# A two-layer graph network: GpSimd clears 256 columns behind every gather, VectorE and ScalarE fetch some chunks by columns, and eleven row buffers are used

## The chip, the cores and the metric

The kernel runs on one core of a Trainium2 chip. The metric is the time of one execution on the device in microseconds (us); lower is better. A core has five engines that run side by side, each with its own instructions in program order, and they wait for one another by semaphores: TensorE (PE: matrix products and transposes into PSUM), VectorE (DVE) and ScalarE (ACT) for work element by element, GpSimd (POOL), and SyncE (SP), which issues DMAs. Here GpSimd issues the indirect DMAs, which fetch rows of a table in device memory by a list of indices.

## The reference

12,500 nodes with 128 features each and 200,000 edges sorted by destination. Layer 1 takes a maximum over the edges of a node, layer 2 a sum.

```python
h = jnp.maximum(_layernorm(x, axis=-1), 0.0)
wsum = segment_sum(edge_weight, dst)
w = edge_weight / jnp.maximum(wsum, EPS)[dst]
feat = relu(h @ W_pool + b_pool)
neigh = segment_max(feat[src] * w[:, None], dst)
neigh = where(deg[:, None] > 0, neigh, 0.0)
rst = h @ W1_self + neigh @ W1_neigh + b1
h1 = relu(rst / jnp.maximum(norm(rst), EPS))
neigh2 = segment_sum(h1[src] * w[:, None], dst) / jnp.maximum(deg, 1.0)[:, None]
out = x + relu(h1 @ W2_self + neigh2 @ W2_neigh + b2)
```

## The kernel before

The edges go in 391 groups of 512 (`G`), each of four chunks of 128 (`Q`). Three stages follow one another.

**Preparation.** The normalised features h are built by columns (feature on the partition, node along the row) in the wide tile `one_way`, which stays on the chip; feat goes to device memory as the table `feat_d`. The first 17 groups (`FIRST`) gather rows of x and finish them themselves, so that layer 1 starts before the table is whole. A generator, `source_steps`, builds the index lists `srcT`.

**Layer 1.** One turn of the loop for each group. `gather` (L513) has GpSimd issue four indirect DMAs, one for a chunk, from `feat_d` into a row buffer `gt` of 128 x 4 x 128. TensorE transposes the chunks into PSUM (`pm`, L964); VectorE multiplies by the edge weights (L1006), runs a scan that takes the maximum along each node's edges (L979), makes a selection (`sel`, L990) and compacts (L999, L1002); TensorE turns the compacted columns (`two_pr`, L1019), ScalarE copies them (`rows`, L974), TensorE multiplies by `sel` (L1028) and ScalarE copies the result to the group's place in a wide tile, at an address that it loaded into a register (L914; registers at L735). VectorE works on several groups' steps in one turn: the program is written as a pipeline, with `due(k)` naming the group k turns back. Work of four nodes' tiles at a time (L796 to L824) turns the result into h1, stored as table `h_d` and kept by columns in `other_way`.

**Layer 2.** GpSimd gathers four chunks of `h_d`; TensorE multiplies each by a small matrix `s` (L1075) that VectorE made from the places and weights (L1063, L1068); VectorE adds the product `pa` to the running sums at a register address (L1080).

What sets the order around the change: each engine's instructions stand in program order; GpSimd's are nearly all gathers. A gather waits until its row buffer is free, that is, until TensorE has read the group that lay there before. `buffer` names the row buffer: layer 1 has a ring of 18 buffers in borrowed space (`ring`), later 14 (`mid`), and from about group 113 the tiles of `full`; layer 2 has `full` alone. `full` holds 11 tiles (`RING` + `MORE`), of which `buffer` uses four (`DEEP`).

Of the kernel before, what the change touches and what calls it, by code (L numbers as in the profile page):

```python
# [7 lines left out]
F32 = mybir.dt.float32  # L8
# [10 lines left out]
P = 128  # L19
# [19 lines left out]
LEAST = LESS + 4 * MID  # L39
KEPT = 4  # L40
# [6 lines left out]
DEEP = 4  # L47
# [3 lines left out]
def gnn_kernel(ctx, tc, x, src, dst, ew, w_pool, b_pool, w1s, w1n, b1, w2s, w2n, b2, out):  # L51
# [31 lines left out]
    s_d = dram.tile([2, NP], F32, name="s_d")  # L83

# [13 lines left out]
    bp_all, b1_all, b2_all = (const.tile([P, D], F32, name=f"b_{i}") for i in range(3))  # L98
    ident = const.tile([P, P], F32)
# [106 lines left out]
    ones_w = rp.tile([P, P], F32)  # L206
    nc.vector.memset(ones_w, 1.0)
# [20 lines left out]
    diff = wk.tile([P, P], F32, bufs=1)  # L228
    nc.gpsimd.iota(diff, pattern=[[1, P]], base=0, channel_multiplier=-1,
# [9 lines left out]
    nc.vector.tensor_scalar(ident, diff, 0.0, None, op0=OP.is_equal)  # L239
    shift = {}  # L240
    for name, at in (("up", 1), ("up_wrap", 1 - P), ("down", -1), ("down_wrap", P - 1)):
        shift[name] = rp.tile([P, P], F32, name=f"shift_{name}")
        nc.vector.tensor_scalar(shift[name], diff, float(at), None, op0=OP.is_equal)
# [264 lines left out]
    def gather(gt, table_d, g, only=None, last=None):  # L508

        t, r, ne, chunks = edges_of(g)  # L510
        limit = {} if last is None else dict(bounds_check=last, oob_is_err=False)
        for j, k in chunks if only is None else chunks[only:only + 1]:
            nc.gpsimd.indirect_dma_start(  # L513
                out=gt[:k, j, :], out_offset=None, in_=table_d[:, :],
                in_offset=bass.IndirectOffsetOnAxis(ap=srcT[:k, t, j, r:r + 1], axis=0), **limit)
        return gt
# [94 lines left out]
    for i in range(len(groups) + 3):  # L611
# [46 lines left out]
        if i < 2 or 9 <= i < 21:  # L658
            next(source_steps, None)
# [31 lines left out]
    def background():  # L691

        for t in range(1, NT):
            yield P * t - 2 * KEPT, edges1, t
        for t in range(NT):
            yield NG, edges2, t
        for t in reversed(range(NT)):
            yield NG, edges3, t
        for t in range(NT):
            yield NG, fitness, t  # L700
        yield NG, lambda get, t: verdict(get), 0

# [168 lines left out]
    with tc.manual_schedule(), tc.tile_pool(name="ew", bufs=3) as wk, \  # L871
# [12 lines left out]
        pms, scs, sels, prs, rws, pas = ({} for _ in range(6))  # L884
        two_pr = ps.tile([P, 2, Q // 2, D], F32, bufs=1)
# [47 lines left out]
        for i in range(max(turn) + 6):  # L933
            if i == NG - 8:
# [9 lines left out]
            if FIRST <= i < NG:  # L944
                gts[i] = gather(buffer(i, True), feat_d, i)
# [5 lines left out]
            if i < FIRST:  # L951
                if i > 0:
                    nc.scalar.activation(pms[i], raws.pop(i).rearrange("p q n -> p (q n)"), AF.Relu, bias=bp_col)
                if i + 1 < FIRST:
                    raw_columns(pn, i + 1)
                if i + 2 < FIRST:
                    raw_scale(i + 2)
                    raw_norm(i + 2)
                if i + 1 < FIRST:
                    raw_back(i + 1)  # L960
            elif i < NG:
                gt = gts.pop(i)
                for j, k in reversed(edges_of(i)[3]):
                    nc.tensor.transpose(pms[i][:, j * P:j * P + k], gt[:k, j, :], ident[:k, :k])  # L964
# [17 lines left out]
            if due(3) is not None:  # L982
                t, r, _, chunks = pairs_of(due(3))
                sel = sels[due(3)] = wk.tile([P, Q // 2, LW], F32, name="sel")
# [7 lines left out]

            pick()
# [47 lines left out]
            if i >= FIRST and i % 3:  # L1041
                side_step()
        assert not busy
# [6 lines left out]
    with tc.manual_schedule(), tc.tile_pool(name="ew2", bufs=3) as wk, \  # L1050
# [6 lines left out]

        nc.vector.memset(agg2, 0.0)
# [66 lines left out]
        for i in range(max(turn) + 2):  # L1125
            if EARLY <= i < NG:
                gts[i] = gather(buffer(i, False), h_d, i)
                places(i)
            if EARLY <= i < NG:
                weighted(i)  # L1130
# [9 lines left out]
            quad_stage(3)  # L1140
            if i in turn:
# [20 lines left out]
            if EARLY <= g < NG:  # L1162
                window_add(g, window_at(mybir.EngineType.DVE, g))
        assert late is None and not quads
# [121 lines left out]
```

## Time and profile before

| | us |
|---|---|
| median of 3 runs | 4587.56 |
| lowest, highest | 4581.83, 4592.94 |
| the profiled execution | 4582.98 |
| its span in the profile | 4581.2 |
| gathers of layer 2 | from about 2372 to 4568 |

The profile is of one execution. A group row of it reads: line, engine, operation, written tile <- read tiles, count | busy us, mean ns of one | idle time of the engine just before them, and what ended most of that. "issue" is waiting for which the profile shows no cause; "remote" is waiting that ended at a semaphore whose giver the profile can't name for that moment. A row of the timeline is: start, duration, engine, line, operation, tiles, and in brackets the idle time ahead of it and what ended it. PE is TensorE's products, PEld its weight loads, which overlap them. A small suffix q (ACTq, DVEq) marks an engine's sequencer, which handles registers and their loads.

### The profile page before, as it was taken

Reading aid. Unit: us, or ns where it says so; the run is one execution under the profiler, and the core shown is the slowest. Engines: PE = TensorE matmul, PEld = TensorE weight load, DVE = VectorE, ACT = ScalarE, POOL = GpSimd, SP = SyncE. Lnnn points to the kernel's source line nnn. Section 1 sums busy time; section 2 is a strip of 40 time slices with the busy share of each in tenths; the row PEclk is TensorE's granted clock in tenths of the full one; section 3 lists DMA queues with packets and bytes.
Section 4 is the critical chain, followed back from the end, with each engine's and each line's share of the span. In section 5 each row is a group of like instructions: output and inputs, shape, how many; then the busy total and the mean of one; then the engine's idle time right before and its main releaser. Section 6 shows DMA issues by size and latency. Waiting matters only on the chain.

```text
span 4581.2 us, 30093 instructions
## 1 busy us (share of the span) xinstructions
PE 1950.3 (43%) x8086; PEld 1623.2 (35%) x8086; DVE 1759.1 (38%) x4405; ACT 422.1 (9%) x1257; POOL 2963.4 (65%) x3143
## 2 busy tenths in 40 slices
PE   3554444444344444443444443333333333333333
PEld 2443334333333333332344433333333333333333
DVE  3676667666666666665561111111111111111111
ACT  3531111111111111111110000000000000000000
POOL 5366664666666666666666666666666666666665
PEclk7765555555555555555555555555555555555555
DMA  4344444444444444443431122211121112112111
GB/s 134 107 117 122 127 120 117 117 119 120 117 119 117 117 120 118 118 121 113 120 96 48 46 57 55 54 51 51 50 56 51 51 51 55 52 51 56 51 51 51
DMA packets 193262, 396.94 MB, mean 87 GB/s; under 512 B 60623, under 2 KB 63822, under 8 KB 193088
## 3 DMA queue, kind: packets, MB, share of 16 engines
q0 software_dynamic: 100032, 204.97, 17.3%
q1 hardware_dynamic: 92320, 189.06, 13.6%
q8 instruction: 69, 1.13, 0.1%
q10 hardware_dynamic: 736, 0.92, 0.1%
q14 instruction: 105, 0.86, 0.1%
HBM read 374.96 MB, written 19.77 MB: 86 GB/s over the span
## 4 chain that ended last, share of the span: by engine, by line
POOL 29%; issue 26%; another core or an unknown queue 19%; DVE 13%; PE 11%; ACT 2%; DMA 1%; POOLq 0%; ACTq 0%; DVEq 0%
POOL gt L513 28%; DVE pm L979 4%; PE pm L964 3%; PE pn L1028 2%; DVE pm L1006 2%; PE two_pr L1019 2%; DVE sc L999 1%; DVE sq L816 1%; DVE sc L1002 1%; DMA gt<-h_d,srcT 1%; PE pa L1075 1%; PE pf L649 1%; ACT rows L974 1%; DVE sel L990 0%
## 5 line engine op out<-in xcount | busy, mean ns | idle before, releaser
L513 POOL DMA_INDIRECT gt<-h_d,srcT x1551 | 1467.7, 946 | 728.9 <-issue 414.2
L513 POOL DMA_INDIRECT gt<-feat_d,srcT x1303 | 1234.9, 948 | 671.8 <-issue 360.7
L1075 PE MATMUL pa<-s,gt 128*128 128x24 f32 x3102 | 716.7, 383 | 1260.4 <-DMA gt<-h_d,srcT 803.5
L1075 PEld LDWEIGHTS pa<-s,gt 128*128 128x128 f32 x3102 | 687.4, 325 | 1328.0 <-issue 813.2
L1080 DVE TENSOR_TENSOR way<-pa,way 128x41 f32 x391 | 77.7, 199 | 1726.2 <-remote 1016.0
L1019 PE MATMUL two_pr<-ident,sc 128*128 128x128 f32 x782 | 243.9, 412 | 942.4 <-ACT rows L974 557.2
L1006 DVE TENSOR_TENSOR pm<-pm,gs 128x512 f32<-128x512 f32 x390 | 271.8, 697 | 680.7 <-remote 428.4
L979 DVE TENSOR_TENSOR_SCAN pm<-kt,pm 128x512 f32<-128x512 bf16 x389 | 499.0, 1283 | 7.1
L1019 PEld LDWEIGHTS two_pr<-ident,sc 128*128 128x128 f32 x782 | 124.9, 201 | 1055.3 <-ACT rows L974 596.0
L964 PE MATMUL pm<-ident,gt 128*128 128x128 f32 x1303 | 323.8, 397 | 99.5 <-issue 54.3
L1028 PEld LDWEIGHTS pn<-sel,rows 128*128 128x128 f32 x1564 | 350.2, 308 | 0.2
L1028 PE MATMUL pn<-sel,rows 128*128 128x48 f32 x1564 | 334.7, 359 | 0.0
L964 PEld LDWEIGHTS pm<-ident,gt 128*128 128x128 f32 x1303 | 243.0, 222 | 135.3 <-issue 87.8
L974 ACT ACTIVATE rows<-two_pr 128x256 f32<-128x256 f32 x392 | 150.4, 384 | 1515.1 <-remote 1046.2
L990 DVE TENSOR_SCALAR sel<-cols,lastT,invT 128x48 f32<-128x48 f32 x782 | 253.4, 324 | 0.0
L832 ACT ACTIVATE oT<-pn,b_col 128x512 f32<-128x512 f32 x24 | 16.5, 689 | 2181.5 <-PE pn L797 701.8
L999 DVE COPY sc<-pm 128x256 f32<-128x256 f32 x391 | 165.8, 424 | 78.8 <-remote 67.3
L1002 DVE COPY_PREDICATED sc<-kt,pm 128x256 f32<-128x256 int16 x389 | 169.3, 435 | 3.9 <-remote 3.9
L513 POOL DMA_INDIRECT w2T<-feat_d,srcT x100 | 94.7, 947 | 97.8 <-DVE raw_mv L527 50.8
L1068 DVE TENSOR_TENSOR s<-place,w2T 128x96 f32<-128x96 f32 x391 | 100.8, 258 | 74.9 <-remote 35.0
L1063 DVE TENSOR_TENSOR place<-place,locT 128x96 f32<-128x96 f32 x391 | 100.9, 258 | 0.3 <-DVE way L1080 0.3
L914 ACT ACTIVATE way<-pn 128x48 f32 x391 | 81.8, 209 | 120.8 <-issue 46.9
(288 smaller groups left out, 1622.8 us busy)
## 6 DMA issues: line engine op xcount, KB each, us to landing
gs<-in_edge_weight SPq DMA_DIRECT2D x389, 256.0 KB
kt<-keep_d SPq DMA_DIRECT2D x97, 512.0 KB
gt<-h_d,srcT POOLq DMA_INDIRECT x1551
gt<-feat_d,srcT POOLq DMA_INDIRECT x1303
feat_d<-fr SPq DMA_DIRECT2D x24, 256.0 KB
xr<-in_x SPq DMA_DIRECT2D x24, 256.0 KB
out<-o SPq DMA_DIRECT2D x24, 256.0 KB
h_d<-sq SPq DMA_DIRECT2D x23, 256.0 KB
```

The lines of the kernel that those rows point to most:

```text
L513: nc.gpsimd.indirect_dma_start(out=gt[:k, j, :], out_offset=None, in_=table_d[:, :], in_offset=bass.IndirectOffsetOnAxis(ap=srcT[:k, t, j, ...
L964: nc.tensor.transpose(pms[i][:, j * P:j * P + k], gt[:k, j, :], ident[:k, :k])
L974: nc.scalar.activation(rws[g][:k, j, :], pr[:k, j, :], AF.Copy)
L979: nc.vector.tensor_tensor_scan(pm[:, :ne], kt[:, :ne], pm[:, :ne], carry, op0=OP.add, op1=OP.max)
L990: nc.vector.tensor_scalar(part, cols[:k, 1, :], lastT[:k, t, j, r:r + 1], invT[:k, t, j, r:r + 1], op0=OP.is_equal, op1=OP.mult)
L999: nc.vector.tensor_copy(sc[:, :ne // 2], two[:, :, 1])
L1002: nc.vector.copy_predicated(sc[:, :ne // 2], new[:, :, 1], two[:, :, 0])
L1006: nc.vector.tensor_tensor(pms[i][:, :n], rows[:, :n], ws.pop(i)[:, :n], OP.mult)
L1019: nc.tensor.transpose(prs[g][:k, j, :], sc[:, j * P:j * P + k], ident)
L1028: nc.tensor.matmul(pas[g], rows[:k, j, :], sel[:k, j, :], start=j == 0, stop=j == len(chunks) - 1)
L1063: nc.vector.tensor_tensor(hit, iota, locT[:, t, :, r:r + 1].to_broadcast([P, Q, PART]), OP.is_equal)
L1075: nc.tensor.matmul(pas[g][:, PART_AT[j]:PART_AT[j] + PART], gt[:k, j, :], s[:k, j, :], start=j == len(chunks) - 1, stop=j == 0, skip_group ...
```

## The change

- Behind every gather, except those of the group 0, GpSimd writes zeros to a tile `spare` of 128 x 256; nothing reads them.
- `buffer` uses all 11 tiles of `full` in both layers.
- A class `Columns` fetches single chunks without GpSimd. The table by columns is on the chip anyway (`one_way` for layer 1, `other_way` for layer 2), and one edge is one column of it. For each chunk SyncE brings a list row with 128 byte addresses (from `at_d`, written in the preparation); the fetching engine loads 16 of them into registers at a time (L755) and copies column after column from the register addresses into the row buffer's slot. ScalarE copies one column with each instruction (128 a chunk, L793). VectorE writes two with each (64 a chunk, L805), the first of them negated.
- Layer 1: VectorE fetches chunk 1 of each 8th group from group 33 on, ScalarE chunk 3 of each 4th from group 29. The columns are of h, not of feat, so TensorE multiplies by `W_pool` instead of a transpose (L1006) and ScalarE adds the bias and cuts at zero (L1011).
- Layer 2: VectorE fetches chunk 1 of each 3rd group from 13 on, ScalarE chunk 2 of each 3.75th. TensorE turns the chunk (`flip`, L1206) and ScalarE copies it back, with the signs put right for VectorE's.
- The preparation computes the address lists (L510). The shift matrices become views of one wider tile, and a bias tile shares its space with `spare`.

In all 361 chunks are fetched by columns (170 by VectorE, 191 by ScalarE), and 2765 gathers are left of 3126.

```diff
+TABLES_AT = (8320, 58688)
+BURST = 16
-DEEP = 4
+REST = 256
...
         if not wide:
-            return full[g % DEEP]
+            return full[g % len(full)]
...
-        return mid[(h - LESS) % MID] if h < LEAST else full[(h - LEAST) % DEEP]
+        return mid[(h - LESS) % MID] if h < LEAST else full[(h - LEAST) % len(full)]
...
             nc.scalar.activation(srcT[:, t], pt, AF.Copy)
+            for layer in range(2):
+                row = (layer * NT + t) * P
+                place = wk.tile([P, G], I32, name="sa")
+                nc.vector.tensor_scalar(place, sr[:, t, :], 4.0, float(TABLES_AT[layer]), op0=OP.mult, op1=OP.add)
+                nc.sync.dma_start(at_d[row:row + P, :], place)
+                yield
...
-    def gather(gt, table_d, g, only=None, last=None):
+    def gather(gt, table_d, g, only=None, last=None, besides=()):
...
         for j, k in chunks if only is None else chunks[only:only + 1]:
+            if any(c.j == j and c.takes(g) for c in besides):
+                continue
             nc.gpsimd.indirect_dma_start(
...
+            if table_d is not x or g > 0:
+                nc.gpsimd.memset(spare, 0.0)
...
+        def load(self, g, _):
+            row = self.layer * NT * P + g
+            nc.sync.dma_start(self.lists[self.place[g]], at_d[row:row + 1, self.j * P:(self.j + 1) * P])
+            self.ready.add(g)
...
+    def one_by_one(slot, r, columns_read):
+        for e, column in enumerate(columns_read, r):
+            by_scalar(slot[:, e:e + 1], column)
...
+    def two_by_two(slot, r, columns_read):
+
+        for e in range(0, BURST, 2):
+            nc.vector.scalar_tensor_tensor(slot[:, r + e:r + e + 2], zero_high, columns_read[e],
+                                           columns_read[e + 1].to_broadcast([P, 2]),
+                                           op0=OP.subtract, op1=OP.min)
...
+        for k, engine, copy, j, every, first in ((0, mybir.EngineType.DVE, two_by_two, 1, 8, FIRST + 16), (1, mybir.EngineType.Activation, one_by_one, 3, 4, FIRST + 12),):
...
-                gts[i] = gather(buffer(i, True), feat_d, i)
+                gts[i] = gather(buffer(i, True), feat_d, i, besides=bycol)
...
+                for c in bycol:
+                    c.turn(i, c.multiplied, c.cut)
                 for j, k in reversed(edges_of(i)[3]):
+                    if any(c.j == j and c.takes(i) for c in bycol):
+                        continue
                     nc.tensor.transpose(pms[i][:, j * P:j * P + k], gt[:k, j, :], ident[:k, :k])
...
+            for c in bycol:
+                c.turn(i, c.load, c.fetch)
...
+        for k, engine, copy, j, every, first in ((0, mybir.EngineType.DVE, two_by_two, 1, 3, 13), (1, mybir.EngineType.Activation, one_by_one, 2, 3.75, 13),):
```

How this moves the instructions. GpSimd in the middle of layer 2, before (`gt_98` and so on are the row buffers; the brackets hold the semaphores that an instruction waits for):

```order
L513 DMA gt_98<-h_d,srcT 128x128 [waits DMASW4_49]
L513 DMA gt_98<-h_d,srcT 128x128 [waits DMASW5_49]
L513 DMA gt_98<-h_d,srcT 128x128 [waits DMASW6_49]
L513 DMA gt_99<-h_d,srcT 128x128 [waits DMASW7_49,PE_49]
L513 DMA gt_99<-h_d,srcT 128x128 [waits DMASW0_49]
L513 DMA gt_99<-h_d,srcT 128x128 [waits DMASW1_49]
```

and now:

```order
L527 DMA gt_106<-h_d,srcT 128x128 [waits DMASW5_49,PE_49]
L531 MEMSET spare 128x256 [waits Pool_49]
L527 DMA gt_106<-h_d,srcT 128x128 [waits DMASW6_49]
L531 MEMSET spare 128x256 [waits Pool_49]
L527 DMA gt_106<-h_d,srcT 128x128 [waits DMASW7_49]
L531 MEMSET spare 128x256 [waits Pool_49]
```

Between two gathers stands a memset, which waits for the memset before it; only a group's first gather waits for TensorE, as before.

VectorE in layer 1, before:

```order
L1006 TENSOR_TENSOR pm<-pm,gs 128x512
L979 SCALAR_TENSOR_TENSOR pm<-kt,pm 128x512
L990 TENSOR_SCALAR sel<-cols,lastT,invT 128x48
L999 COPY sc<-pm 128x256
L990 TENSOR_SCALAR sel<-cols,lastT,invT 128x48
L1002 COPY_PREDICATED sc<-kt,pm 128x256
```

and now, where L1145, L1116, L1127, L1138 and L1141 are the same steps (the scan is L979 before and L1116 now):

```order
L1145 TENSOR_TENSOR pm<-pm,gs 128x512
L805 SCALAR_TENSOR_TENSOR gt_104<-ends,way_65 128x2 x8
L1116 SCALAR_TENSOR_TENSOR pm<-kt,pm 128x512
L755 TENSOR_LOAD listed
L1127 TENSOR_SCALAR sel<-cols,lastT,invT 128x48
L1138 COPY sc<-pm 128x256
L1127 TENSOR_SCALAR sel<-cols,lastT,invT 128x48
L1141 COPY_PREDICATED sc<-kt,pm 128x256
```

An eighth of a chunk stands in each turn, between the multiplication and the scan, and the load of the next 16 registers behind the scan.

ScalarE in layer 1, before:

```order
L914 ACTIVATE way_65<-pn 128x48
L974 ACTIVATE rows<-two_pr 128x256
L735 TENSOR_LOAD bases
L914 ISA
L914 ACTIVATE way_65<-pn 128x48
```

and now, where L1111 is the copy `rows` (L974 before) and L1045 the copy to the group's place (L914 before):

```order
L1045 ACTIVATE way_66<-pn 128x48
L793 ACTIVATE gt_99<-way_65 128x1 x16
L755 TENSOR_LOAD listed
L793 ACTIVATE gt_99<-way_65 128x1 x16
L755 TENSOR_LOAD listed
L1011 ACTIVATE pm<-pm,bp_col 128x128
L1111 ACTIVATE rows<-two_pr 128x256
L849 TENSOR_LOAD bases
L1045 ISA
L1045 ACTIVATE way_66<-pn 128x48
```

Two bursts of 16 columns, each with a register load behind it, have come between the copies of one group and those of the next.

More of the change, by code (lines that the diff above doesn't have):

```diff
@@ L39 @@
 LEAST = LESS + 4 * MID
+TABLES_AT = (8320, 58688)
+BURST = 16
+HIGH = 1.0e30
 KEPT = 4
@@ L1125, in gnn_kernel @@
         for i in range(max(turn) + 2):
+            for c in bycol:
+                c.turn(i, c.load)
             if EARLY <= i < NG:
-                gts[i] = gather(buffer(i, False), h_d, i)
+                gts[i] = gather(buffer(i, False), h_d, i, besides=bycol)
                 places(i)
+            for c in bycol[:1]:
+                c.ahead()
+                c.fetch_one(i)
             if EARLY <= i < NG:
@@ L1140, in gnn_kernel @@
             quad_stage(3)
+            for c in bycol[:1]:
+                c.ahead()
+                c.fetch_one(i)
             if i in turn:
```

130 lines of the change are left out of this document (119 added, 11 removed).

## The prediction

> **What bounds the kernel now.** I read the page's busy shares and its chain first, then the groups of GpSimd's gathers, then its waits by layer, and last the timeline around one wait.
>
> ```profile
> PE 1950.3 (43%) x8086; PEld 1623.2 (35%) x8086; DVE 1759.1 (38%) x4405; ACT 422.1 (9%) x1257; POOL 2963.4 (65%) x3143
> POOL 29%; issue 26%; another core or an unknown queue 19%; DVE 13%; PE 11%; ACT 2%; DMA 1%; POOLq 0%; ACTq 0%; DVEq 0%
> L513 POOL DMA_INDIRECT gt<-h_d,srcT x1551 | 1467.7, 946 | 728.9 <-issue 414.2
> ...
> L513 POOL DMA_INDIRECT gt<-feat_d,srcT x1303 | 1234.9, 948 | 671.8 <-issue 360.7
> ```
>
> GpSimd leads, and nearly all it does is gathers: 946 to 948 ns each. The chain gives it 29% and 26% to "issue", which is the gap that follows a gather. Layer 2 (1551 gathers, 388 groups of four) takes 1467.7 + 728.9 = 2196.6 us, which is **5.66 us for a group**. Its idle time divides so:
>
> ```profile
> POOL gt L513 <- issue: 412.1, 1352, 0.3
> POOL gt L513 <- remote: 276.6, 98, 5.7
> ```
>
> 1352 gathers follow the one before after 0.30 us, so the pace is 0.946 + 0.305 = 1.25 us, 5.0 for a group. 98 times GpSimd waits longer: 276.6 - 98 x 0.3 = 247 us, 0.64 for a group. One such wait, on GpSimd, TensorE and VectorE:
>
> ```profile
> 3014.38 0.95 POOL L513 DMA_INDIRECT gt<-h_d,srcT  x1 [0.30 <-issue]
> 3020.29 0.95 POOL L513 DMA_INDIRECT gt<-h_d,srcT  x1 [4.96 <-remote]
> ```
>
> ```profile
> 3012.00 1.87 PE L1075 MATMUL pa<-s,gt 128*128 128x24 f32 x8 [3.19 <-DMA gt<-h_d,srcT]
> ```
>
> ```profile
> 3003.96 0.20 DVE L1080 TENSOR_TENSOR way<-pa,way 128x41 f32 x1 [9.39 <-PE pa L1075]
> ...
> 3020.05 0.20 DVE L1080 TENSOR_TENSOR way<-pa,way 128x41 f32 x1 [15.43 <-remote]
> 3020.17 0.26 DVE L1063 TENSOR_TENSOR place<-place,locT 128x96 f32<-128x96 f32 x1
> 3020.46 0.26 DVE L1068 TENSOR_TENSOR s<-place,w2T 128x96 f32<-128x96 f32 x1
> 3020.64 0.19 DVE L1080 TENSOR_TENSOR way<-pa,way 128x41 f32 x1
> ```
>
> TensorE's products were done at 3013.87; VectorE, which adds them, went on only at 3020.05, and then added several groups in a row. In between GpSimd ran out of free buffers at 3015.33. So TensorE's work was finished and its signal came late, after the gathers had stopped. I call this a **hold-up**; why it occurs the trace doesn't say.
>
> Layer 1 shows the same on VectorE:
>
> ```profile
> 1713.20 0.30 DVE L990 TENSOR_SCALAR sel<-cols,lastT,invT 128x48 f32<-128x48 f32 x1
> 1713.41 0.44 DVE L1002 COPY_PREDICATED sc<-kt,pm 128x256 f32<-128x256 int16 x1
> 1713.74 0.70 DVE L1006 TENSOR_TENSOR pm<-pm,gs 128x512 f32<-128x512 f32 x1
> ...
> 1716.76 0.69 DVE L1006 TENSOR_TENSOR pm<-pm,gs 128x512 f32<-128x512 f32 x1
> ...
> 1731.73 0.70 DVE L1006 TENSOR_TENSOR pm<-pm,gs 128x512 f32<-128x512 f32 x1 [8.14 <-remote]
> ```
>
> A group takes it 3.02 us when nothing is late, then it waits 8.14. By stages (stretch, length, busy time and count of TensorE's products, its weight loads, VectorE, ScalarE and GpSimd, then clock, DMA share and GB/s):
>
> ```profile
> 186.00:700.00 514.00, 244.63 (x1012) 189.54 (x1012) 332.87 (x703) 95.48 (x291) 331.08 (x349) 0.58 0.41 116
> 720.00:1500.00 780.00, 355.61 (x1544) 286.07 (x1544) 504.09 (x943) 105.09 (x344) 493.42 (x521) 0.56 0.42 118
> 1500.00:2347.00 847.00, 368.05 (x1602) 295.31 (x1602) 521.23 (x1040) 100.50 (x344) 562.41 (x594) 0.57 0.42 119
> 3400.00:4560.00 1160.00, 434.95 (x1736) 384.25 (x1736) 134.45 (x628) 8.27 (x12) 773.34 (x818) 0.50 0.20 53
> ```
>
> GpSimd's counts by four are groups: 87.25, 130.25 and 148.5 in layer 1, so 5.89, 5.99 and 5.70 us a group; I take 5.8. In the third stretch VectorE is busy 3.51 of a group and ScalarE 0.68. In layer 2 (818 gathers, 204.5 groups) VectorE is busy 0.66 a group and ScalarE 0.04.
>
> **The change part by part.** Times are against the profiled execution, 4582.98 us (span 4581.2); the median of three runs is 4.6 us higher.
>
> *Fewer gathers.* With a chunk left out in each 8th and each 4th group a layer-1 group has 4 - 1/8 - 1/4 = 3.625 gathers; in layer 2, 4 - 1/3 - 1/3.75 = 3.4. That concerns some 357 groups of layer 1 (33 to 389) and 373 of layer 2 (13 to 385).
>
> *The clearing of 256 columns behind each gather.* The nearest rows are GpSimd's small operations, one of them between gathers:
>
> ```profile
> 20.80 0.95 POOL L513 DMA_INDIRECT gt<-in_x,srcT  x1 [0.30 <-issue]
> 21.74 0.12 POOL L626 MEMSET way<- 128x1 f32 x1
> 22.05 0.94 POOL L513 DMA_INDIRECT gt<-in_x,srcT  x1 [0.19 <-issue]
> ...
> 35.82 0.10 POOL L626 MEMSET way<- 128x1 f32 x1 [6.57 <-ACT xn L622]
> 36.07 0.94 POOL L513 DMA_INDIRECT gt<-in_x,srcT  x1
> ```
>
> ```profile
> L626 POOL MEMSET way<- 128x1 f32 x7 | 0.8, 115 | 6.6 <-ACT xn L622 6.6
> L229 POOL IOTA diff<- 128x128 f32 x1 | 0.2, 233 | 0.4 <-POOLq L1267 0.4
> ...
> L236 POOL IOTA need<- 128x4 f32 x1 | 0.1, 130 | 0.0
> L246 POOL IOTA late_nodes<- 128x4 f32 x1 | 0.1, 130 | 0.0
> L238 POOL MEMSET way<- 128x48 f32 x1 | 0.1, 128 | 0.0
> ```
>
> A 0.12 us memset begins as the gather ends, and the next gather still comes 1.25 us after the last: it hides in the 0.30 gap. After the second one a gather follows at 36.07, 0.15 behind the memset's end. From 128x1 to 128x48 a memset grows by 13 ns in 47 columns, so 256 columns are 115 + 255 x 0.28 = 0.19 us. Iota grows by 103 ns in 124 columns; by its slope 256 columns are 0.34. So the gap becomes 0.19 + 0.15 = 0.34 (a period of 1.29) or 0.34 + 0.15 = 0.49 (1.44); at best the gap hides it (1.25). I take the row of the same operation, **1.29**: 4.68 us a group in layer 1, 4.39 in layer 2.
>
> *VectorE's columns.* A chunk is 64 instructions of 128x2, with two scalar columns at register addresses. No row has that shape. A 128x41 addition at a register address is followed by the next operation after 0.12 us (3020.05, 3020.17), and L990, which takes two scalar columns, after 0.21 (1713.20, 1713.41). I take 0.13, since the size is small: 8.3 us a chunk, within 7.7 and 13.4. Layer 1: 3.51 + 8.3/8 = 4.55 a group (5.2 at the upper end). Its eight loads of registers stand behind the scan there, which covers them. In layer 2 they have little beside them:
>
> ```profile
> L979 DVE TENSOR_TENSOR_SCAN pm<-kt,pm 128x512 f32<-128x512 bf16 x389 | 499.0, 1283 | 7.1
> ```
>
> ```profile
> L735 ACTq TENSOR_LOAD <-bases x49: 537/547/982, 200.1 to 2350.4; - x49
> L735 DVEq TENSOR_LOAD <-bases x49: 594/596/1054, 2386.5 to 4544.7; - x49
> ```
>
> The scan runs 1.28 us and a load 0.6. So layer 2 gives VectorE 0.66 + 8.3/3 = 3.43, and up to 8 x 0.6/3 = 1.6 more if no load is covered.
>
> *ScalarE's columns.* A chunk is 128 instructions of 128x1.
>
> ```profile
> 1701.86 0.39 ACT L974 ACTIVATE rows<-two_pr 128x256 f32<-128x256 f32 x1 [8.84 <-remote]
> 1702.14 0.21 ACT L914 ACTIVATE way<-pn 128x48 f32 x1
> ```
>
> ```profile
> L768 ACT ACTIVATE ss<-ss 128x1 f32<-128x1 f32 x6 | 1.2, 204 | 0.2
> ```
>
> One of 128x1 lasts 0.204; but the 0.39 us operation at 1701.86 is followed by the next after 0.28, so 0.11 of it lies under its successor. 0.204 - 0.11 = 0.09; I take 0.10, between that and the full 0.204: 12.8 us a chunk (26.1 without overlap). Layer 1: 0.68 + 12.8/4 = 3.9, with its eight loads uncovered 5.0; layer 2: 0.04 + 12.8/3.75 = 3.45, with the loads 4.6. The Trainium skill (ScalarE: Activation LUTs, What ACT_TABLE_LOAD costs) states 186 ns plus 0.833 a column, with about 93 ns overlapped: an estimate of 94 ns a column, 12.0 us a chunk, and then the sum would be the same, since GpSimd stays the slowest; the trace's 204 ns and 0.11 agree roughly.
>
> *The waits it adds.* A register load waits for its list row, which SyncE requests two turns (about 10 us) ahead; behind it stand all later columns and, on ScalarE, the copies L974 and L914 of layer 1. TensorE's product of a fetched chunk waits for VectorE or ScalarE; behind it stand the next groups' products. Both come free if the fetching engine keeps its pace, which the terms above price, and else cost what that engine is late.
>
> *Eleven buffers, and the rest.* More buffers let GpSimd run over a hold-up of some groups. The clearing may also end the hold-ups; the trace can't show it, as before has no clearing in these stages. TensorE gets a product or a transpose back for each fetched chunk, nothing that counts at 43% busy. The address lists cost eight VectorE operations of 128x512, at the 0.70 of the one at 1713.74: 6 us if all lie on the path.
>
> *Sum.* Layer 1's three engines come to 4.68, 4.55 and 3.9 to 5.0, so near one another that each will wait for the others now and then; I take 5.0, adding 0.3. Layer 2's are 4.39, 3.4 to 5.0 and 3.5 to 4.6; I take 4.6, which also leaves 0.2 of the 0.64 for hold-ups. (5.8 - 5.0) x 357 = 286 and (5.66 - 4.6) x 373 = 395; less the 6: 675. 4583 - 675 = 3908, and I say **3910**. Of this the missing gathers alone, 361 x 1.25 = 451, are the larger part.
>
> **Rivals.**
>
> *Everything hides.* Clearing within the gap, no hold-up left: layer 1 at VectorE's 4.55, layer 2 at 3.4 x 1.25 = 4.25. (1.25 x 357) + (1.41 x 373) = 972: about 3610. For it speaks the memset at 21.74; against it, that VectorE then has no slack in layer 1.
>
> *The clearing is long.* At iota's slope, 1.44: 5.22 and 4.90, so 207 + 283 = 490 less: about 4100.
>
> *The hold-ups stay* (slower). Then VectorE's columns, which stand behind its waiting instruction in program order, are done after the wait and not in it. Layer 1 gets 5.8 + 1.04 = 6.84: +371; layer 2 gains nothing, as more buffers only put off the stop that ends a hold-up. About 4950. It decides if over half of layer 2's waits of 4 to 5 us remain. For it: in the wait shown, as in others, the signal comes only after the gathers have stopped. Against it: the stretch from 186 to 700, with 18 and 14 buffers, ran at 5.89 us a group, and with four it was 5.99 and 5.70, so that depth alone did not lengthen them; and the clearing puts other work where a gather followed a gather.
>
> *ScalarE becomes the bound* (slower). At the full 0.204 with loads: layer 1 0.68 + 26.1/4 + 1.1 = 8.3, layer 2 0.04 + 26.1/3.75 + 1.2 = 8.2: 2.5 x 357 + 2.5 x 373 = 1840 more, 6400. The point of balance is 0.13 us a column ((5.66 - 1.2) x 3.75 / 128). Against it: the 0.28 between two starts where the first lasts 0.39.
>
> *The fetches hold the gathers.* If VectorE's instructions kept GpSimd from its descriptors, each chunk's 8.3 us would be added to the gathers: 4.39 + 2.77 = 7.2 in layer 2, +570 there, 1.04 in layer 1, about 5100. In the trace the gather at 3020.29 lasts 0.95 with VectorE busy beside it, as at 3014.38 with VectorE idle. The Trainium skill (SBUF — State Buffer, Who interferes with whom) has VectorE operations with two SBUF inputs contend with GpSimd instructions that read SBUF, though not with those that only write, so the clearing would be free of it; by that rule the gathers would suffer, and the trace's two rows disagree.
>
> **How the numbers follow.** My forecast 0.45, everything hides 0.18, long clearing 0.20, hold-ups 0.10, ScalarE 0.05, held gathers 0.02. The forecast's own range is 3700 to 4080. The first three, 0.83, are faster; of the hold-ups some could end near no change. Faster by over 0.2% (9 us, about what a measurement here can tell from no change) 0.83, within it 0.02, slower 0.15. The range goes from 3600 (everything hides) up to where both unknown prices are high at once: VectorE at 0.21 a column pair with no load of layer 2 covered would take 0.66 + 13.4/3 + 1.6 = 6.7 a group there, +1.0 x 373 against before, while layer 1 at 5.22 still gains 207: 4750. That needs every bound together; a third of the way from 4100 to it is 4300, two thirds 4530. I end at 4450; what lies above is about 0.15, below about 0.05.
>
> **What would show it.** Gathers of 0.95 with a period of 1.29 in steady stretches (1.25 or 1.44 for the rivals); about 2765 gathers; waits of GpSimd over 1 us summing to under 100 us in layer 2; L805 every 0.13 us and L793 every 0.10 in a burst; layer 1 at 5.0 and layer 2 at 4.6 us a group. I am wrong if TensorE's signals still come in bursts after the gathers stop, or if ScalarE is busy over 90% of a stage.

## The result, and the profile after

| | us |
|---|---|
| before, median of 4 runs | 4584.69 |
| changed, median of 4 runs | 4647.14 (4635.26 to 4661.12) |
| changed against before | 1.0135, 95% interval 1.0096 to 1.0174 |
| span of the changed kernel's profiled run | 4659.3 (before 4581.2) |

The change made the kernel slower by 1.35%; the forecast was 3910 us, and 4647 lies above its range.

The page of the changed kernel: the busy shares, the chain, and the groups that answer to those shown of before.

```profile
PE 2064.4 (44%) x8447; PEld 1711.1 (37%) x8447; DVE 3255.7 (70%) x15295; ACT 3212.3 (69%) x26111; POOL 3549.1 (76%) x5543
ACT 56%; issue 25%; PE 8%; DVE 5%; ACTq 3%; POOL 1%; DMA 0%; another core or an unknown queue 0%; DVEq 0%; SPq 0%; POOLq 0%
L793 ACT ACTIVATE gt<-way 128x1 f32 x23040 | 2579.3, 191 | 951.5 <-issue 910.0
L805 DVE SCALAR_TENSOR_TENSOR gt<-ends,way 128x2 f32<-128x2 f32 x10560 | 1534.3, 215 | 352.3 <-issue 327.9
L527 POOL DMA_INDIRECT gt<-h_d,srcT x1326 | 1264.5, 954 | 479.4 <-issue 202.8
L527 POOL DMA_INDIRECT gt<-feat_d,srcT x1183 | 1131.8, 957 | 398.8 <-PE pm L1101 214.1
...
L531 POOL MEMSET spare<- 128x256 f32 x2761 | 910.3, 330 | 2.1
```

The chain has changed hands: ScalarE has 56% of it, where GpSimd led before; GpSimd has 1%. ScalarE's columns take 2579.3 us and the idle time ahead of them 951.5, together 0.153 us a column. A clearing takes 330 ns. The waits of GpSimd, over the whole run and then in layer 2 alone, in us, times and longest:

```profile
POOL gt L527 <- issue: 390.3, 2330, 1.5
POOL gt L527 <- PE pm L1101: 214.1, 86, 18.3
POOL gt L527 <- PE pa L1231: 138.0, 60, 7.4
POOL gt L527 <- PE flip L1206: 130.5, 47, 7.6
POOL r_f L527 <- DVE ends L815: 79.8, 1, 79.8
```

```profile
POOL gt L527 <- issue: 202.8, 1215, 0.6
POOL gt L527 <- PE pa L1231: 138.0, 60, 7.4
POOL gt L527 <- PE flip L1206: 130.5, 47, 7.6
...
POOL gt L527 <- remote: 0.6, 1, 0.6
```

Layer 2's 276.6 us of "remote" (the hold-ups) have gone to 0.6. But GpSimd waits no less: its waits of over 1 us there, under whatever label, sum to 271 us in 75 waits before and to 261 us in 77 now. In place of "remote" stand 138.0 and 130.5 us of waiting for TensorE's products and turns, and TensorE in turn waits for ScalarE:

```profile
PE pa L1231 <- ACT gt L793: 1154.4, 166, 20.9
ACT gt L793 <- issue: 932.5, 2793, 5.8
```

In layer 1 TensorE waits for ScalarE's copies, which stand behind its columns in program order. Below that wait are two stretches from the middle of the layer, in the columns of the forecast's table by stages:

```profile
PE two_pr L1158 <- ACT rows L1111: 410.3, 140, 9.3
```

```profile
720.00:1500.00 780.00, 374.46 (x1510) 293.30 (x1508) 619.89 (x1983) 565.44 (x4644) 608.44 (x949) 0.53 0.39 112
1500.00:2300.00 800.00, 376.16 (x1527) 293.62 (x1527) 619.01 (x2050) 576.76 (x4760) 636.44 (x990) 0.54 0.38 111
```

Half of GpSimd's 949 and 990 instructions are clearings; at 3.625 gathers a group that is 5.96 and 5.86 us a group.

And there is a wait that before doesn't have: one of 79.8 us, near the start, of a gather into the buffer `r_f` for VectorE's `ends`. The span grew by 78.1.

ScalarE's and GpSimd's timelines over the same 5 us of layer 2:

```profile
3600.31 1.62 ACT L793 ACTIVATE gt<-way 128x1 f32 x16
3602.08 0.37 ACT L793 ACTIVATE gt<-flip,ends 128x128 f32<-128x128 f32 x1
3602.36 0.39 ACT L793 ACTIVATE gt<-way 128x1 f32 x3
3603.10 0.48 ACT L793 ACTIVATE gt<-way 128x1 f32 x4 [0.35 <-issue]
3603.83 0.30 ACT L793 ACTIVATE gt<-way 128x1 f32 x2 [0.25 <-issue]
3604.55 0.48 ACT L793 ACTIVATE gt<-way 128x1 f32 x4 [0.43 <-issue]
3605.29 0.39 ACT L793 ACTIVATE gt<-way 128x1 f32 x3 [0.25 <-issue]
```

```profile
3600.97 0.95 POOL L527 DMA_INDIRECT gt<-h_d,srcT  x1 [0.16 <-issue]
3601.92 0.33 POOL L531 MEMSET spare<- 128x256 f32 x1
3602.41 0.95 POOL L527 DMA_INDIRECT gt<-h_d,srcT  x1 [0.16 <-issue]
```

Sixteen columns in 1.62 us is the forecast's price, 0.10. But from 3602.36 on two to four come every 0.73 us, some 0.23 each, with no cause that the profile names. GpSimd's period is 0.95 + 0.33 + 0.16 = 1.44 us.

### The profile page after: what moved, and what is told of

It reads as the page before. It is cut to its first block, busy times and chain, and to the rows that moved or that the text cites. A ratio compares the mean times of both kernels' runs of the same rounds, so it can differ in the third digit from the quotient of the medians.

```text
span 4659.3 us, 72554 instructions
## 1 busy us (share of the span) xinstructions
PE 2064.4 (44%) x8447; PEld 1711.1 (37%) x8447; DVE 3255.7 (70%) x15295; ACT 3212.3 (69%) x26111; POOL 3549.1 (76%) x5543
## 4 chain that ended last, share of the span: by engine, by line
ACT 56%; issue 25%; PE 8%; DVE 5%; ACTq 3%; POOL 1%; DMA 0%; another core or an unknown queue 0%; DVEq 0%; SPq 0%; POOLq 0%
ACT gt L793 48%; ACTq L755 3%; ACT w2T L793 1%; ACT way L1045 1%; DVE sq L930 1%; PE pn L910 1%; ACT rows L1111 1%; ACT pm L1011 1%; PE pf L665 1%; PE pn L911 1%; POOL gt L527 1%; PE pm L1101 1%; DVE pm L1116 1%; PE pa L1231 1%; PE pm L1006 1%
## 5 line engine op out<-in xcount | busy, mean ns | idle before, releaser
L793 ACT ACTIVATE gt<-way 128x1 f32 x23040 | 2579.3, 191 | 951.5 <-issue 910.0
L805 DVE SCALAR_TENSOR_TENSOR gt<-ends,way 128x2 f32<-128x2 f32 x10560 | 1534.3, 215 | 352.3 <-issue 327.9
L527 POOL DMA_INDIRECT gt<-h_d,srcT x1326 | 1264.5, 954 | 479.4 <-issue 202.8
L527 POOL DMA_INDIRECT gt<-feat_d,srcT x1183 | 1131.8, 957 | 398.8 <-PE pm L1101 214.1
L531 POOL MEMSET spare<- 128x256 f32 x2761 | 910.3, 330 | 2.1
L1158 PE MATMUL two_pr<-near_ones,sc 128*128 128x128 f32 x782 | 252.2, 424 | 750.2 <-ACT rows L1111 410.3
L1116 DVE TENSOR_TENSOR_SCAN pm<-kt,pm 128x512 f32<-128x512 bf16 x389 | 498.5, 1282 | 0.2
L1145 DVE TENSOR_TENSOR pm<-pm,gs 128x512 f32<-128x512 f32 x390 | 270.4, 693 | 310.4 <-ACT rows L1111 122.2
L1158 PEld LDWEIGHTS two_pr<-near_ones,sc 128*128 128x128 f32 x782 | 128.6, 205 | 871.3 <-ACT rows L1111 468.8
L1127 DVE TENSOR_SCALAR sel<-cols,lastT,invT 128x48 f32<-128x48 f32 x782 | 283.9, 364 | 221.4 <-PE pn L1167 191.6
L1101 PE MATMUL pm<-near_ones,gt 128*128 128x128 f32 x1183 | 314.3, 412 | 171.7 <-ACT pm L1011 93.1
L1101 PEld LDWEIGHTS pm<-near_ones,gt 128*128 128x128 f32 x1183 | 230.8, 233 | 221.6 <-ACT pm L1011 113.4
L1111 ACT ACTIVATE rows<-two_pr 128x256 f32<-128x256 f32 x392 | 148.8, 380 | 65.8 <-issue 57.6
L1141 DVE COPY_PREDICATED sc<-kt,pm 128x256 f32<-128x256 int16 x389 | 167.8, 431 | 0.0
L1138 DVE COPY sc<-pm 128x256 f32<-128x256 f32 x391 | 162.2, 415 | 0.1
L1045 ACT ACTIVATE way<-pn 128x48 f32 x391 | 81.9, 209 | 113.1 <-PE pn L911 87.5
L1006 PE MATMUL pm<-gt,w_pool 128*128 128x128 f32 x240 | 89.2, 474 | 140.1 <-ACT pm L1011 118.6
```

Source lines behind the costliest of these rows:

```text
L527: nc.gpsimd.indirect_dma_start(out=gt[:k, j, :], out_offset=None, in_=table_d[:, :], in_offset=bass.IndirectOffsetOnAxis(ap=srcT[:k, t, j, ...
L531: nc.gpsimd.memset(spare, 0.0)
L793: nc.scalar.activation(out, in_, AF.Copy, **scale)
L805: nc.vector.scalar_tensor_tensor(slot[:, r + e:r + e + 2], zero_high, columns_read[e], columns_read[e + 1].to_broadcast([P, 2]), op0=OP.su ...
L1111: nc.scalar.activation(rws[g][:k, j, :], pr[:k, j, :], AF.Copy)
L1116: nc.vector.tensor_tensor_scan(pm[:, :ne], kt[:, :ne], pm[:, :ne], carry, op0=OP.add, op1=OP.max)
```

## The experiments

Each set ran on one chip, with the kernel before beside it. What before took there turned out to matter, so the table has it. The five sets ran on five different chips, each once, so what is said of a chip below could also belong to its surroundings at the time.

| set, before on that chip | kernel | us | against before, 95% interval |
|---|---|---|---|
| 1, 4619.62 | no clearing | 5315.95 | 1.1497 (1.1476 to 1.1519) |
| | no columns | 4666.32 | 1.0096 (1.0077 to 1.0115) |
| | columns by VectorE only | 4559.24 | 0.9872 (0.9852 to 0.9891) |
| | half of ScalarE's | 4585.82 | 0.9934 (0.9916 to 0.9952) |
| 2, 3945.18 | no columns, clearing 64 | 4133.75 | 1.0475 (1.0458 to 1.0493) |
| | no columns, clearing 1 | 4034.79 | 1.0226 (1.0209 to 1.0243) |
| | no columns, four buffers | 4624.50 | 1.1715 (1.1696 to 1.1735) |
| | one gather a group in layer 2 (three of four left out) | 3830.11 | 0.9706 (0.9687 to 0.9726) |
| 3, 3952.93 | as changed | 4112.99 | 1.0411 (1.0394 to 1.0429) |
| | as before | 3953.42 | 1.0003 (0.9993 to 1.0014) |
| | no columns, clearing 1 | 4040.94 | 1.0224 (1.0207 to 1.0241) |
| | eleven buffers alone | 4033.68 | 1.0210 (1.0193 to 1.0227) |
| 4, 3945.91 | signs late | 4030.68 | 1.0215 (1.0201 to 1.0229) |
| | signs late, no clearing | 3618.17 | 0.9166 (0.9152 to 0.9180) |
| | signs late, no columns, clearing 1 | 3956.67 | 1.0029 (1.0018 to 1.0039) |
| | signs late, clearing 1 | 3627.42 | 0.9192 (0.9178 to 0.9206) |
| 5, 4587.07 | signs late, no columns, clearing 1 | 4613.60 | 1.0062 (1.0045 to 1.0079) |
| | signs late, clearing 64 | 5183.59 | 1.1307 (1.1281 to 1.1333) |

**No clearing.**

```diff
-            if table_d is not x or g > 0:
-                nc.gpsimd.memset(spare, 0.0)
```

> The changed kernel without the clearing behind the gathers; columns and eleven buffers stay. Theory A (the clearing ends the hold-ups of TensorE's signals): they return, GpSimd's waits put down to 'remote' rise to over 200 us, and the time goes above 4750 us. Rival (the clearing only lengthens the gather's period and something else ended the hold-ups): no such waits, the period falls from 1.445 to 1.25 us, and the time stays within 50 us of 4647, since ScalarE's columns set the pace in either case.

5315.95 us: by the ratios to before, 13% above the changed kernel. GpSimd's waits in that run, and TensorE's for the columns:

```profile
POOL gt L527 <- PE pa L1229: 748.2, 154, 9.2
POOL gt L527 <- PE pm L1099: 747.0, 173, 32.6
...
POOL gt L527 <- remote: 89.9, 46, 14.0
```

```profile
PE pa L1229 <- ACT gt L791: 1325.0, 160, 15.5
```

Theory A holds in the time, but this run does not show its mechanism: the waits are put down to TensorE and not to "remote", and TensorE in turn waits for ScalarE's columns. The clearing is worth more than it costs here. ScalarE's columns were slower still; their group in that run:

```profile
L791 ACT ACTIVATE gt<-way 128x1 f32 x23040 | 2534.3, 191 | 1515.5 <-issue 1499.2
```

(2534.3 + 1515.5) / 23040 = 0.176 us a column, against 0.153 with the clearing. So what the clearing relieves includes ScalarE; what it does to TensorE's signals, the kernel without columns shows better.

**No columns; VectorE only; half of ScalarE's.** The three change the intervals of the two fetching engines; a `first` of NG stands for never.

```diff
# columns by VectorE only
-(0, mybir.EngineType.DVE, two_by_two, 1, 8, FIRST + 16), (1, mybir.EngineType.Activation, one_by_one, 3, 4, FIRST + 12)
+(0, mybir.EngineType.DVE, two_by_two, 1, 8, FIRST + 16), (1, mybir.EngineType.Activation, one_by_one, 3, 4, NG)
-(0, mybir.EngineType.DVE, two_by_two, 1, 3, 13), (1, mybir.EngineType.Activation, one_by_one, 2, 3.75, 13)
+(0, mybir.EngineType.DVE, two_by_two, 1, 3, 13), (1, mybir.EngineType.Activation, one_by_one, 2, 3.75, NG)
# half of ScalarE's: its intervals 4 -> 8 and 3.75 -> 7.5
# no columns: NG for both engines
```

> Clearing and eleven buffers, but no chunk fetched by columns: all gathers stay with GpSimd. If the clearing ends the hold-ups, GpSimd alone sets the pace: 4 x 1.445 = 5.78 us a group in both layers, about 4640 us, no more than 50 us of waits over 1 us in layer 2. If it does not, some 250 us a layer of hold-ups come on top: about 5100.

> Only VectorE fetches columns; ScalarE fetches none. Theory S (ScalarE's columns are the bound of the changed kernel, at about 0.166 us each with their stalls): GpSimd sets the pace, 3.875 x 1.445 = 5.60 us a group in layer 1 and 3.667 x 1.445 = 5.30 in layer 2, about 4450 us. Rival (VectorE's columns or the clearing cost the time): not below 4600.

> ScalarE fetches half as many chunks: each 8th group in layer 1, each 7.5th in layer 2. Theory S: GpSimd sets the pace, 3.75 x 1.445 = 5.42 and 3.533 x 1.445 = 5.11 us a group, about 4350 us. Rival (ScalarE's columns delay TensorE's groups whatever their number, by their waits in program order): about 4600.

Without columns the time is 4666.32, within 30 us of the expectation, and GpSimd waits for little but its own gap and once for `ends`:

```profile
POOL gt L527 <- issue: 479.6, 2877, 0.6
POOL r_f L527 <- DVE ends L815: 83.2, 1, 83.2
POOL w2T L527 <- DVE raw_mv L543: 32.2, 1, 32.2
```

No wait of GpSimd in layer 2 is over 1 us, where before had 75 on the chip of the result. So the clearing, with eleven buffers, removes the hold-ups without the help of columns, and its 0.195 us at each gather costs as much as they did. With VectorE's columns only, 4559.24: faster than the changed kernel and than before, which supports theory S, but 110 us short of its number; with half of ScalarE's 4585.82, short by 236. The number assumed that GpSimd sets the pace as soon as ScalarE does not. In the VectorE-only run VectorE's group reads:

```profile
L805 DVE SCALAR_TENSOR_TENSOR gt<-ends,way 128x2 f32<-128x2 f32 x10560 | 1597.1, 216 | 560.9 <-issue 522.8
```

(1597.1 + 560.9) / 10560 = 0.204 us for a pair, against 0.13 in the forecast: VectorE's columns too stall where nothing is waited for, so it is the next to be late.

**Shorter clearings, four buffers, fewer gathers.**

```diff
-                nc.gpsimd.memset(spare, 0.0)
+                nc.gpsimd.memset(spare[:, :64], 0.0)
# or spare[:, :1]; four buffers: full[g % 4], full[(h - LEAST) % 4] with the clearing of 256
# one gather a group in layer 2, with all columns:
-            if any(c.j == j and c.takes(g) for c in besides):
+            if any(c.j == j and c.takes(g) for c in besides) or table_d is h_d and besides and j > 0:
```

> No columns, eleven buffers, and the clearing cut from 256 to 64 columns. By the 330 ns of 256 columns and the 115 of one, 64 are 0.17 us and the period 0.95 + 0.17 + 0.16 = 1.28 us. Theory P (any instruction between two gathers lets TensorE's signals through): hold-ups stay away, layer 2 takes 4 x 1.28 = 5.1 us a group, and the time is about 4300 us. Rival L (the length of the pause does it): they return in part, and the time is 4500 or more.

> As the one before, with a clearing of one column, which hides in the gap: period 1.25 us. Theory P: 5.0 us a group, about 4250 us. Rival L: the hold-ups are there in full, with eleven buffers to fill before each ends, 4600 us or more.

> No columns, clearing of 256 columns, and four row buffers in place of eleven. If the clearing alone ends the hold-ups, the number of buffers counts for nothing: 4666 us within 20, as with eleven. If eleven buffers are part of the remedy, over 4750.

> The changed kernel, but layer 2 leaves out three of a group's four gathers (chunk 0 alone is gathered; chunk 3, and the others where no engine fetches them, hold what lay there). Theory G (running gathers hold back the engines that fetch columns): in layer 2 a column of ScalarE falls from 0.166 us to 0.12 or less and an instruction of VectorE's from 0.196 to 0.14, and a group from 5.6 to about 4.2 us. Rival (their own register loads, or each other, hold them back): 0.16 and 0.19 stay, and a group stays at 5.4 or more.

On this chip before itself took 3945.18, 14% less than on the first, so that none of the four could tell what it was meant to. The first three measure the clearing: each shows nearly nothing but GpSimd's period.

```profile
L531 POOL MEMSET spare<- 128x64 f32 x3122 | 528.7, 169 | 2.2
```

```profile
L531 POOL MEMSET spare<- 128x1 f32 x3122 | 371.5, 119 | 1.2
```

169 - 119 = 50 ns for 63 columns, 330 - 119 = 211 for 255: 0.8 ns a column, iota's slope and not the 0.28 that the forecast took. The kernel with one gather a group had ScalarE's columns near 0.105 us apart, by their starts, as theory G wants, and a group of layer 2 at 4.2 us, but the next set shows that they cost that on such a chip with all the gathers too: it tells nothing. One comparison with set 1 does tell something: with the clearing of 256 and no columns the time is 4624.50 here (four buffers) and was 4666.32 there (eleven), 1% apart, where before differs by 17%.

**Both kernels once more, and the parts, on one chip.**

> The changed kernel once more, with the kernel before on the same chip, to see whether the comparison itself depends on the chip. Theory K (the hold-ups belong to some chips or to their surroundings): where before takes about 3945 us, this one goes at GpSimd's longer period, 3.4 x 1.445 = 4.91 us a group in layer 2 and about 4.9 in layer 1, some 4080 us, slower than before by 3 to 4%; where before takes 4580 to 4620, it takes about 4650. Rival (the low times of before on the second chip had another cause, such as the clock): the ratio to before stays near 1.01 wherever it runs.

> The kernel before once more, for its profile on this chip. Theory K: at about 3945 us its layer 2 has under 50 us of GpSimd's waits over 1 us and 5.0 us a group; at about 4600 us it has some 250 us of them and 5.6 us. Rival: the waits are alike at both times and the gather's own time differs from 0.946 us.

> No columns, eleven buffers, clearing of one column, as before. On a chip where before takes about 4600 us: theory P (any instruction between the gathers ends the hold-ups) 4050 us, rival L (only a long pause does) 4600 or more. On a chip where before takes about 3945 us: 4035 us again, which tells nothing of the two.

> No columns, no clearing, eleven buffers. On a chip with hold-ups: more buffers let each hold-up run on until they are full; theory D (depth makes it worse) over 4750 us, rival (depth covers part of it) 4550 or less. On a chip without: GpSimd's pace, 4 x 1.25 us a group, about 3960 us, as before.

Theory K holds: 4112.99 (4080 expected), 4.1% slower than before, which took 3952.93. Layer 1 took 5.25 us a group (539 gathers from 720 to 1500 us, 3.625 a group) and layer 2 4.91 (1385 gathers and clearings from 2400 to 3400 us, 3.4 gathers a group). Layer 2 of before on this chip, GpSimd's waits:

```profile
POOL gt L513 <- issue: 436.7, 1433, 0.3
POOL gt L513 <- DMA gt<-h_d,srcT: 34.4, 113, 0.3
POOL gt L513 <- PE pa L1075: 0.9, 3, 0.3
```

No wait is over 0.3 us. The same instructions, with no hold-up. The changed kernel's columns on this chip:

```profile
L793 ACT ACTIVATE gt<-way 128x1 f32 x23040 | 2289.5, 190 | 46.0 <-issue 32.7
L805 DVE SCALAR_TENSOR_TENSOR gt<-ends,way 128x2 f32<-128x2 f32 x10560 | 1514.0, 215 | 287.4 <-issue 270.6
```

(2289.5 + 46.0) / 23040 = 0.101 us a column, where the chip of the result had 0.153. So ScalarE's stalls belong to the same chips as TensorE's late signals. Eleven buffers alone took 4033.68, 81 above before, and its profile has the wait for `ends` too:

```profile
POOL r_f L527 <- DVE ends L813: 81.8, 1, 81.8
```

**The signs late.** `sign_tiles` makes a tile of signs in the scratch `f1`, which is the row buffer of group 19. GpSimd issues that gather long before VectorE comes to turn 17.

```diff
-            if i == FIRST:
+            if i == FIRST + 4:
                 sign_tiles(work("f1")[:, :P])
```

> The changed kernel with the tile of signs made four turns later, after the gather of group 19, whose row buffer it uses as scratch. Theory W (the one wait of about 80 us of GpSimd on VectorE near the start is due to that scratch): the wait goes, and the time falls by 70 to 85 us against the changed kernel, to about 4030 us where before takes 3950, and to about 4570 where it takes 4590 to 4620. Rival (the wait is made up for later, since other engines are the bound): less than 20 us of it shows.

> The same without the clearing. Where before takes about 3950 us (no hold-ups): GpSimd's period falls to 1.25 us and the columns take their part off it; VectorE is next in layer 2 at 0.66 + 64 x 0.185 / 3 = 4.6 us a group, layer 1 at 3.625 x 1.25 = 4.53: about 3700 us. Where before takes 4590 or more: hold-ups return as in the run without clearing, about 5230.

> No columns, eleven buffers, clearing of one column, the signs late. Where before takes 4590 or more: theory P (any instruction between the gathers ends the hold-ups) about 3960 us; rival L (only a long pause does) 4500 or more. Where before takes 3950: the same 3955, and the two stay untold.

> The changed kernel with the signs late and a clearing of one column. Where before takes 4590 or more: by P the period of 1.25 us helps only GpSimd, ScalarE stays the bound at about 0.166 us a column, some 4550 us; by L the hold-ups return, about 5200. Where before takes 3950: about 3700, as without the clearing.

4030.68 us is 82 less than the changed kernel took in set 3, where before took nearly the same (77 less by the ratios), and the wait for `ends` is not in its profile: theory W holds. Without the clearing as well the time is 3618.17, and with a clearing of one column 3627.42: where no hold-ups occur the columns bring 8%, more than the expected 3700 us has it. Layer 2 of the run without clearing:

```profile
L527 POOL DMA_INDIRECT gt<-h_d,srcT x1326 | 1252.8, 945 | 404.1 <-issue 330.7
```

(1252.8 + 404.1) / 388 = 4.27 us a group, GpSimd's pace of 3.4 x 1.25. The forecast's rival "everything hides" said 3610.

**Short clearings where the hold-ups occur.** The kernel "signs late, no columns, clearing 1" again, and "signs late" with `memset(spare[:, :64], 0.0)`.

> No columns, eleven buffers, clearing of one column, signs late, once more, for a chip with hold-ups if one is met. Where before takes 4590 or more: theory P (any instruction between the gathers ends the hold-ups) about 3960 us; rival L (only a long pause does) 4500 or more. Where before takes 3950: 3957 again.

> The changed kernel with the signs late and a clearing of 64 columns: period 1.28 us. Where before takes 4590 or more: if 64 columns keep the hold-ups away, ScalarE's columns are the bound and the time is 4550 us; if not, about 5000. Where before takes 3950: GpSimd 3.4 x 1.28 = 4.35 us a group in layer 2 and 4.64 in layer 1, some 30 to 80 us above the 3627 of one column, about 3690.

On this chip before took 4587.07, and the first of the two 4613.60: rival L. GpSimd's waits in its layer 2 are those of before again:

```profile
POOL gt L527 <- issue: 277.1, 1399, 1.6
POOL gt L527 <- remote: 202.9, 75, 4.9
POOL spare L531 <- remote: 48.2, 48, 2.6
```

And with the columns and a clearing of 64, the columns stall nearly as without a clearing, and the time is 5183.59 us, a little over the 5000 expected:

```profile
L793 ACT ACTIVATE gt<-way 128x1 f32 x23040 | 2532.8, 191 | 1462.5 <-issue 1448.8
```

(2532.8 + 1462.5) / 23040 = 0.173 us a column. An instruction between the gathers is not enough; 0.12 us (alone) and 0.17 us (with columns) do not do it, 0.33 does.

## Why the prediction was wrong

**Bound of before: right.** The hold-ups are what keeps layer 2 from GpSimd's pace: where they do not occur, before takes 3945 to 3953 us, some 640 less, with no wait over 0.3 us. I took them for a trait of the kernel. They came on the chip of the result and in sets 1 and 5 (before took 4580 to 4620 there), and not in sets 2 to 4.

**ScalarE's price: the step that failed.** "I take 0.10" for a column, and the rival "ScalarE becomes the bound" got a chance of 0.05, with the balance at 0.13. The burst bears the 0.10 out, and so does set 3 with 0.101 for all columns. But the chip of the result gave 0.153, past the balance: 128 x 0.153 = 19.6 us a chunk, 5.2 a group of layer 2, and with the copies back and the waits for TensorE's turns it goes at 1264.5 + 479.4 + 1326 x 0.33 = 2181.5 us for 388 groups, 5.62 where I had 4.6 and before had 5.66. I priced an instruction from two rows, each in a stretch where ScalarE had little to do, and never asked whether what delayed TensorE's signals would delay ScalarE's instructions. Layer 1 failed in the same way: 5.96 and 5.86 us a group where I had 5.0 and took 5.8 for before, with TensorE waiting for the copies behind the columns. There I had also priced a load of 16 registers with the row of eight: it takes 1.02 us and not 0.55, so that eight loads, if uncovered, are 2.0 us a group and not 1.1. The sign that I named for this rival, ScalarE busy over 90% of a stage, did not come (67 to 72%), because stalled time is not counted as busy.

The runs bear out the size of it. In set 3, where a column cost what I took, the changed kernel took 4112.99 us, at 5.25 and 4.91 us a group: the rival "the clearing is long" said 5.22 and 4.90. As far as two chips can be compared, 534 of the 737 us by which the forecast missed go with the stalls, and the other 203 with the long clearing and one wait of 80 us. But leaving ScalarE's columns out does not win the 534 back, since GpSimd then has more gathers to do and VectorE's columns stall (below).

That the stalls and the late signals have one cause is shown only as far as this: both occur on the same chips and both are absent on the others, and both are worse without the clearing (0.176 us a column, and 89.9 us of "remote" in place of 0.6). In the changed kernel's layer 2 the starts of columns are on average 0.178 us apart while gathers follow one another, and 0.118 once none has begun for 1.55 us (10,668 and 2,126 starts; gaps of 1.3 us and more left out). Within bursts of 16 they are 0.138 apart in layer 1 and 0.154 in layer 2, and 0.093 and 0.094 in set 3.

What the cause is stays open. One thing more goes with it in every run: the traces from the chips with hold-ups lack about half to three quarters of the records of semaphore updates, all along the span. That of before holds 17,526, that of the same program in set 3 70,323; no trace of the result or of sets 1 and 5 holds more than 37,342, and none of sets 2 to 4 fewer than 55,716. So part of what stands as "remote" or "issue" there may be missing records. Each time on record comes with a span and a clock out of such a recording, so a rival that no run here tests is that the recording itself delays the engines on those chips.

**The clearing: mis-sized, and better than I allowed.** It takes 0.330 us, not 0.19; the period is 1.445, the rival "the clearing is long", not 1.29. On the other hand it does end the hold-ups, which I left half open: without columns no wait over 1 us remains in layer 2. With them the sign I named, under 100 us of such waits, failed at 261, but these are waits for TensorE behind ScalarE's columns. Its cost and its gain cancel nearly (no columns: 1.0096, with the 83 us wait for `ends` in it).

**A wait that I missed.** The scratch of the signs is a row buffer that GpSimd wants: 79.8 us once, more than the loss of 62.5 us between the medians. I listed the waits that the change adds and left this one out, though the change has `sign_tiles` write `work("f1")` in turn 17 and `buffer` shows who else uses it.

**VectorE's price: right in a burst, low in layer 2.** Two bursts in the changed kernel's layer 2:

```profile
3603.31 1.14 DVE L805 SCALAR_TENSOR_TENSOR gt<-ends,way 128x2 f32<-128x2 f32 x8 [0.69 <-issue]
3604.37 0.26 DVE L1219 TENSOR_TENSOR place<-place,locT 128x96 f32<-128x96 f32 x1
3604.80 1.22 DVE L805 SCALAR_TENSOR_TENSOR gt<-ends,way 128x2 f32<-128x2 f32 x8 [0.17 <-issue]
```

Seven steps and one of 0.215 in 1.14 us are 0.13 a pair, the price taken; but idle time stands between bursts, and over the run a pair costs (1534.3 + 352.3) / 10560 = 0.179. On the chip of set 3 it is (1514.0 + 287.4) / 10560 = 0.171, so this is mostly not the hold-ups. Of the idle time 296 us stand ahead of the first pair of a burst, where the register load is, and 57 within bursts (in set 3 285 and 2). So the uncovered loads are the likely cause; that was not tested by itself. The forecast bounded them at 1.6 us a group of layer 2, with 0.6 us a load; at 1.10 the bound is 2.9. In the kernel with VectorE's columns only it is otherwise: 330 us of its 560.9 stand within bursts, whose pairs start 0.192 us apart in layer 2 and not 0.13. VectorE stalls there as ScalarE does, and the kernel gained only 2.6% on the changed one, by their ratios to before, and not 4.

**Buffers, gathers, the other rivals.** Eleven buffers alone do nothing where no hold-ups occur (4033.68, less the wait 3952, as before); alone on a chip with hold-ups they were not run, only with the clearing of one column, where they bring nothing either (1.0062). The fetches do not hold the gathers: 954 and 957 ns against 946 and 948. The hold-ups did not stay, so that rival is wrong; the run without the clearing (5315.95) went past its 4950, but by ScalarE's stalled columns and not as the rival has it.

So on the chip of the result gains and losses nearly cancel: 361 gathers fewer and the hold-ups gone on one side, the clearing and ScalarE's late columns on the other. The 80 us wait would tip it to slower; the changed kernel without that wait was not run on such a chip, so this is not shown. On a chip without hold-ups the clearing only costs, and the change is 4.1% slower; without the clearing and the wait it was 8% faster there (0.9166). No version was run that is faster than before on both kinds of chip: VectorE's columns only took 0.9872 of before in set 1, and were not run elsewhere.

## What to carry to other kernels

When an engine that waits for little is given thousands of small instructions, its price may not be that of a burst: ask first what already delays other engines in that stage, and price it at the balance too, with a real chance. A scratch tile that is lent from a pool of buffers makes the pool's engine wait for the borrower, however short the work; look up who takes that buffer next, and how far ahead that engine runs. And run before on more than one chip ahead of tuning against a wait whose cause the profile cannot name, and look whether the traces of both hold as many semaphore updates.

## What was not expected of the hardware

The same program took 3945 to 3953 us on three chips and 4580 to 4620 on others, at granted clocks of 0.544 and 0.547, with layer 2's gathers of 0.944 and 0.946 us. GpSimd was busy for 2958.6 and 2963.4 us, so for it the whole difference is idle time. Without columns, a pause of 0.33 us behind each gather removed the long waits, and one of 0.12 us left 202.9 us of "remote" in layer 2. A load of 16 registers took 1.02 us on ScalarE and 1.10 on VectorE, against 0.55 and 0.60 for the eight of before:

```profile
L755 ACTq TENSOR_LOAD <-listed x1528: 1002/1020/1543, 245.7 to 4624.2; - x191
L755 DVEq TENSOR_LOAD <-listed x1360: 1093/1098/1631, 248.0 to 4616.3; - x195
```
